# Merging each attention group with the image while the next groups run, in a four-layer image kernel on one core

## The chip, the cores and the metric

The kernel runs on one core of a Trainium2 chip. The metric is device microseconds of one execution; the kernel before takes 5507.82 us, the median of 3 runs (5503.45 to 5507.88).

## What is computed

The input x has 2 images of 128 channels, 128 rows (h) and 128 columns (w), in float32. Four layers follow each other, each on the group-normalised output of the one before, and each added to it (pre-activation residual):

```python
x = x + axial_attention(_gn(x))      # layer 0: along h, for every column w
x = x + four_line_scans(_gn(x))      # layer 1: down, up, right, left
x = x + deformable_conv(_gn(x))      # layer 2
x = x + hadamard_conv(_gn(x))        # layer 3
```

The change is in layer 0 and at the start of layer 1. Layer 0, for each of the 256 columns (image n, column w) and each of 8 groups of 16 channels:

```python
qkv = _bn(einsum('bgch,gdc->bgdh', xg, wg))             # q, k: 8 channels, v: 16
stacked = _bn(concat([qk, qr, kr]))                     # logits: q*k, q*embedding, k*embedding
sim = softmax(stacked.sum(over the three terms))
sv  = einsum('bgij,bgcj->bgci', sim, v)                 # "sums"
sve = einsum('bgij,cij->bgci', sim, v_emb)              # "embedded"
so  = _bn(concat([sv, sve]))                            # statistics per channel, over all columns and rows
out = so.reshape(N, W, 128, 2, H).sum(axis=3)           # sv and sve of a channel added
```

`_bn` of the output takes its mean and variance per channel over both images. A channel belongs to one group, so a group's output scales are known as soon as that group is done for both images. Layer 1 then takes the group norm of x + out (statistics over the whole image, 4 channels together) and runs four scans of 128 lines: each line is the line of the input plus the relu of a 9-tap convolution of the line before.

## The kernel before

The program is written for a tile framework. Where an engine is wrapped in `InOrder` (the helper of line 81, to which most instructions are put down in the profile), its instructions run in the order of the Python code; elsewhere the framework's scheduler picks the order. Matrix multiplies run on PE, vector work on DVE, activations on ACT, elementwise work also on POOL; DMAs are issued by SP in its own program order, a few by ACT.

**Preparing (`layer0_prepare`, line 92).** After the statistics, the last part (from line 493) loops over 32 blocks of four rows. Each step t makes q and k by position for the moments of the logits (`positions`, `against_embeddings`), and from t = 4 to t = 32 it also issues `project`: one matmul `ps_q` of 128x512, and two ACT activations of it into `sa` and `sb`; there are 64 projections, two to three a step, `ps_q` has two PSUM buffers. Every 4 projections `sb` goes to DRAM (`qb`, 1 MB), every 8 `sa` goes to DRAM (`qa`, 2 MB). The scales of the logits (`alphas`) come after the last step.

**Attention (`layer0_attention`, line 612).** A unit is 32 columns of one image and one group; there are 64 units (2 images, 8 groups, 4 blocks of 32 columns), with the image as the outermost loop. A unit is done in four pairs of 8 columns. The loop over m (line 865) runs 256 pairs and 15 more turns that drain the pipeline; turn m issues, in this order: logits of pair m (PE `lg`, then DVE `e<-lg,r`), the first half of the turning of pair m-2 (PE `te`, DVE `et<-te`), the maxima of pair m (DVE `mx`), the division of pair m-1 (DVE reciprocal of `total`, POOL `e<-e,total`), values of pair m-3 (PE `po`, ACT `svt<-po`), terms of the next unit (PE `gen`, ACT and DVE `r<-gen`), the embedded sums of pair m-7 (PE `po`, ACT `ste<-po`), the second half of the turning, the copy by position (POOL `et<-et`), and the 8 exponentials of pair m (ACT `e<-e,mx`). DVE's `bn_stats` of `svt` and `ste` follow, four for each unit. At the end of a turn come SP's transfers: at m % 4 == 3 the loads of `zz` (16 DMAs of 16 KB, two buffers) and `vt` for the unit after the next, and the stores of `svt` and `ste` (4 DMAs each) of finished units; at m % 4 == 0 the loads of `qk` (4 DMAs).

**Merging (`Merge`, line 929).** `Merge.begin` is called when the last logits are issued; `Merge.run` (line 1007) follows when attention has ended: `scales` makes the two factors and the shift per channel, then 8 blocks of 32 columns are read back from DRAM, scaled (ACT `u`), added (DVE `te`), added to the image in SBUF (`res`, half on DVE, half on POOL) and measured by `bn_stats` (DVE).

**First scan (`layer1`, line 1101).** `res` is stored to DRAM (`x1_d`, 34 DMAs), copied there once more by blocks of columns (`x1c_d`, 64-byte pieces, needed by the fourth scan alone), the group norm's scales are made, and scan d = 0 runs from row 0 to row 127, with rows normalised by ACT four rows ahead.

Of the kernel before, what the change touches and what calls it, by code (L numbers as in the profile page):

```python
# [16 lines left out]
N = 2  # L17
# [74 lines left out]
def layer0_prepare(env, x, prm, mem, alphas):  # L92
# [10 lines left out]
    with ExitStack() as ctx:  # L103
# [389 lines left out]
        with ExitStack() as part:  # L493
# [35 lines left out]
            def against_embeddings(t, zs):  # L529
# [20 lines left out]
                nc.gpsimd.tensor_tensor(acc, acc, prod, ALU.add)  # L550
# [26 lines left out]
            wait = 4  # L577
            zs_last = None
            for t in range(NT + 1):
                zs = positions(t) if t < NT else None  # L580
                if t >= wait:
                    share = -(-len(todo) // (NT + 1 - t))
                    for n, wc, b in todo[:share]:
# [5 lines left out]
                        if b % 4 == 3:  # L589
                            nc.sync.dma_start(  # L590
                                out=mem["qb"][:, n, wc, b // 4 * 2 : b // 4 * 2 + 2], in_=sb
                            )
                        if b == NB - 1:
                            nc.sync.dma_start(out=mem["qa"][:, n, wc], in_=sa)
# [17 lines left out]
def layer0_attention(env, prm, mem, alphas, mv, then):  # L612
# [20 lines left out]
    with ExitStack() as ctx:  # L633
# [7 lines left out]
        pp = ctx.enter_context(tc.tile_pool(name="at_ps", bufs=1, space=PSUM))  # L641

        st_v, st_e = (
            cp.tile([P, NG, N * NC, 2, 6], F32, name=f"st_so{k}", tag=f"st_so{k}")
# [3 lines left out]
        nc.scalar.dma_start(out=ve, in_=prm["vemb"])  # L648
# [3 lines left out]
        for j in range(2):  # L652
            nc.gpsimd.memset(zz[j].rearrange("p t i b w -> p (t i b w)"), 0.0)
        qk = zp.tile([P, 2, HW, S], F32, name="qk", tag="qk")
        po = pp.tile([P, 256], F32, name="po", tag="po")
        nc.vector.memset(po, 0.0)
        po_v = po.rearrange("p (q i) -> p q i", q=2)
        po_e = po.rearrange("p (i w) -> p i w", w=WC)

        qb = mem["qb"].rearrange("(t g c) n e s i b w -> g n e (s i) c t (b w)", t=2, g=NG)  # L660
        qa = mem["qa"].rearrange(
            "(t g c) n e (q r x) h -> t g c n e r q (x h)", t=2, g=NG, r=2, x=RT
        )
        sv = mem["sv"].rearrange("(g c) n e (q x) h -> g x c n e q h", g=NG, x=RT)
        sve = mem["sve"].rearrange("(g c) n e (s i) w -> g s c n e (i w)", g=NG, s=4)

        units = [(n, g, wc) for n in range(N) for g in range(NG) for wc in range(NC)]
# [4 lines left out]
        def load(at):  # L672
# [4 lines left out]
            for i in range(16):  # L677
                sync.dma_start(
# [8 lines left out]
        def load_qk(u):  # L687
            for t in range(2):
                for r in range(2):
# [3 lines left out]
                        in_=qa[t, u.g, :, u.n, u.wc, r],  # L693
                    )

        def terms_pe(u, t, k):
# [15 lines left out]
        def terms_copy(u, t, k, ps, s):  # L712

            part = slice(0, 1) if s == 0 else slice(1, 4)
# [4 lines left out]
            if s == 0:  # L719
                dve.tensor_scalar(to, here, scale, None, ALU.mult)  # L720
            else:
                act.activation(to, here, AF.Copy, scale=scale)
# [29 lines left out]
        def add_term(u, p, lg):  # L752
            e = ep.tile([P, 2 * RT, S], F32, name="e", tag="e", bufs=4)
# [48 lines left out]
        def values(u, p, et):  # L802
# [10 lines left out]
            if p == 0:  # L813
                u.sv = sp.tile([P, 2 * RT, S], F32, name="svt", tag="svt")
            act.copy(u.sv[:, 2 * p : 2 * p + 2, :], po_v)
# [19 lines left out]
        def store_sv(u):  # L835
            for x in range(4):
                sync.dma_start(out=sv[u.g, x, :, u.n, u.wc], in_=u.sv[32 * x : 32 * x + 16])

        def store_sve(u):
            for s in range(4):  # L840
                sync.dma_start(
                    out=sve[u.g, s, :, u.n, u.wc],
# [3 lines left out]
        def stats(u, st, t, half):  # L846
            dve.bn_stats(
                st[:, u.g, u.n * NC + u.wc, half, :],
                t.rearrange("p a b -> p (a b)")[:, 512 * half : 512 * half + 512],
# [7 lines left out]
        for at in range(2):  # L857
            us[at] = load(at)
            load_qk(us[at])
        for t in range(2):  # L860
            for k in range(2):
                ps = terms_pe(us[0], t, k)
                for s in (0, 1):
                    terms_copy(us[0], t, k, ps, s)
        for m in range(pairs + 15):
            here = m < pairs
            if m == pairs:
                early.close()
                then()
# [18 lines left out]
            if nxt and here:  # L888
                ps = terms_pe(nxt, p // 2, p % 2)
                for s in (1, 0):  # L890
                    terms_copy(nxt, p // 2, p % 2, ps, s)
# [1299 lines left out]
```

## Time and profile before

| | |
|---|---|
| median of 3 runs | 5507.82 us |
| profiled execution, its own time | 5498.68 us |
| its span | 5496.8 us |
| busy over the span | PE 94%, DVE 67%, ACT 49%, POOL 28% |
| first `gen` matmul, first `lg` matmul of attention | 399.8 us, 420.8 us |
| last `mx` of attention | 1892.3 us |
| last statistics of attention done | 1919.8 us |
| first matmul of the first scan | 2060.0 us |
| last matmuls of the four scans | about 3690 us |

A profile is one execution. A row of a timeline gives the start, the duration, the engine, the output and inputs, and in brackets how long the engine had been idle and who released it. A row of a stretch gives, for each engine, busy time and the number of instructions, then the share of full clock that PE was granted, the mean busy share of the 16 DMA engines and the rate. Busy times of pipelined instructions overlap a little, so the distance between starts is often shorter than the duration.

### The profile page before, as it was taken

Reading aid. Unit: us, or ns where it says so; the run is one execution under the profiler, and the core shown is the slowest. Engines: PE = TensorE matmul, PEld = TensorE weight load, DVE = VectorE, ACT = ScalarE, POOL = GpSimd, SP = SyncE. Lnnn points to the kernel's source line nnn. Section 1 sums busy time; section 2 is a strip of 40 time slices with the busy share of each in tenths; the row PEclk is TensorE's granted clock in tenths of the full one; section 3 lists DMA queues with packets and bytes.
Section 4 is the critical chain, followed back from the end, with each engine's and each line's share of the span. In section 5 each row is a group of like instructions: output and inputs, shape, how many; then the busy total and the mean of one; then the engine's idle time right before and its main releaser. Section 6 shows DMA issues by size and latency. Waiting matters only on the chain. (4 is left out here: it accounts for less than half of the span.)

```text
span 5496.8 us, 172767 instructions
## 1 busy us (share of the span) xinstructions
PE 5176.2 (94%) x72443; PEld 4608.0 (84%) x72443; DVE 3663.1 (67%) x7010; ACT 2672.4 (49%) x8182; POOL 1565.9 (28%) x1235
## 2 busy tenths in 40 slices
PE   7889999999999809999999999999899999999999
PEld 6757888888888709999999999984799999999877
DVE  3637888888888775555555556653566666666788
ACT  3558998888888745552223320013233333333332
POOL 3215666666666641000000003330000000000476
PEclk8999999999999859999999999999999999999999
DMA  4352333333333399900000001004667666666111
GB/s 162 136 234 52 61 61 61 61 61 61 61 61 61 96 366 167 93 1 1 1 1 1 1 1 47 32 34 122 110 88 88 88 88 87 88 88 88 41 55 55
DMA packets 673354, 421.04 MB, mean 77 GB/s; under 512 B 325696, under 2 KB 630720, under 8 KB 660672
## 3 DMA queue, kind: packets, MB, share of 16 engines
q1 hardware_dynamic: 667406, 400.69, 38.8%
q8 instruction: 580, 9.50, 0.7%
q10 hardware_dynamic: 5170, 9.23, 0.5%
q14 instruction: 198, 1.62, 0.1%
HBM read 269.09 MB, written 157.45 MB: 78 GB/s over the span
## 5 line engine op out<-in xcount | busy, mean ns | idle before, releaser
L81 PE MATMUL pl<-ln,wl 128*128 128x128 f32 (+1 forms) x10160 | 1240.7, 276 | 9.4 <-DVE ln L81 7.9
L81 PEld LDWEIGHTS pl<-ln,wl 128*128 128x128 f32 x10160 | 1175.7, 190 | 22.3 <-issue 6.6
L81 ACT ACTIVATE e<-e,mx 128x128 f32<-128x128 f32 x2048 | 793.4, 395 | 0.8 <-DVE mx L81 0.8
L81 ACT COPY sm<-ps_s 128x432 f32<-128x432 f32 (+1 forms) x768 | 318.2, 487 | 833.3 <-PE ps_s L81 808.9
L81 ACT COPY res<-ln 128x64 f32<-128x64 f32 (+1 forms) x1016 | 283.9, 304 | 701.5 <-DVE ln L81 701.5
L81 POOL TENSOR_TENSOR e<-e,total 128x1024 f32<-128x1024 f32 x256 | 485.6, 1897 | 486.3 <-DVE total L81 481.4
L81 DVE COPY s<-ps_w 100x1152 f32<-100x1152 f32 x256 | 346.3, 1353 | 333.4 <-PE ps_w L81 326.6
L81 POOL TENSOR_TENSOR res<-ln,x1t 128x128 f32<-128x128 f32 x256 | 148.9, 582 | 1428.7 <-DVE ln L81 1428.7
L81 PE MATMUL ps_s<-s,xw 100*128 100x144 f32 x4096 | 546.5, 287 | 6.6 <-DMA xw<-px_d 6.6
L81 PE MATMUL po<-sm,wdef 128*128 128x256 f32 x2304 | 539.2, 379 | 0.0
L81 PE MATMUL pl<-ln,ws 128*128 128x128 f32 x4064 | 536.8, 273 | 0.0
L81 POOL COPY et<-et 128x1024 f32<-128x1024 f32 x256 | 517.2, 2020 | 34.9 <-DVE et L81 26.1
L81 PEld LDWEIGHTS ps_s<-s,xw 100*128 100x128 f32 x4096 | 518.5, 191 | 7.1 <-DMA xw<-px_d 7.0
L81 DVE TENSOR_TENSOR v<-pl,c 128x128 f32<-128x128 f32 x508 | 148.0, 291 | 540.5 <-PE pl L81 537.3
L81 PEld LDWEIGHTS pl<-ln,ws 128*128 128x128 f32 x4064 | 494.5, 190 | 0.0
L81 ACT ACTIVATE r<-gen,alphas 128x1536 f32<-128x1536 f32 x256 | 394.9, 1542 | 172.3 <-PE gen L81 144.2
L81 PEld LDWEIGHTS po<-sm,wdef 128*128 128x128 f32 x2304 | 419.8, 190 | 47.6
L81 POOL MEMSET col<- 128x10 f32 (+1 forms) x72 | 5.9, 122 | 1460.6 <-DVE res L81 1453.0
L81 ACT ACTIVATION_READ_ACCUMULATOR e<-e,mx 128x1 f32 x2048 | 396.8, 194 | 0.0
L81 DVE SCALAR_TENSOR_TENSOR ln<-v,res 128x128 f32<-128x128 f32 x1016 | 346.4, 341 | 48.5 <-POOL res L81 0.9
L81 PE MATMUL te<-cst_main,e 128*128 128x128 f32 x2048 | 338.6, 288 | 24.0 <-POOL e L81 16.7
L81 PE MATMUL gen<-zz,toep 32*128 32x128 f32 x8192 | 334.1, 288 | 23.2 <-DMA zz<-qb_d 15.2
(247 smaller groups left out, 9118.8 us busy)
## 6 DMA issues: line engine op xcount, KB each, us to landing
xw<-px_d SPq DMA_DIRECT2D x1275, 80.0 KB
xa<-in_x SPq DMA_DIRECT2D x16, 1024.0 KB
v_d<-vs SPq DMA_DIRECT2D x16, 1024.0 KB
qb_d<-sb SPq DMA_DIRECT2D x16, 1024.0 KB
qa_d<-sa SPq DMA_DIRECT2D x8, 2048.0 KB
zz<-qb_d SPq DMA_DIRECT2D x1024, 16.0 KB
vt<-v_d SPq DMA_DIRECT2D x64, 256.0 KB
qk<-qa_d SPq DMA_DIRECT2D x256, 64.0 KB
```

Of the source, the lines that this page charges most:

```text
L81: return lambda *a, **k: self.tc.keep_in_program_order(issue(*a, **k))
```

## The change

In attention the group becomes the outermost loop (`units`), so that a group is complete for both images after 32 pairs. A new method `Merge.slot(m, ...)` is called at the end of every turn m. For group g it issues, from turn 32g + 43 on, the scales of that group in five steps (two small DVE operations; a matmul into 4 columns of `po`; four DVE operations; a square root on ACT; five DVE operations), and then, for 7 of the 8 groups, eight chunks (image, 32 columns) at a distance of three turns: loads of `te`, `tv` and of the image chunk `t` into SBUF, one ACT activation of 128x512, three POOL operations of 128x512, one DVE `bn_stats`, and the store of the merged chunk to `x1_d`. The last group is merged after attention in `Merge.finish`. `Merge.norm` makes the group norm's scales from the statistics by group. `res` isn't filled any more by merging: `layer1` loads it row block by row block from `x1_d`.

The DRAM tensors change their layout: `qa`, `qb` and `x1_d` have image and block before the channel; `sv` has pieces of 16 floats where it had 128, so that the channels of a group and eighths of the rows make 128 partitions; `te`, `tv` are read as 2 KB per partition, the image chunk in pieces of 32 floats. The projections are done in turns 4 to 27, three in a turn. The first unit's loads of `zz` are shared by the queues of SP and ACT, and its four `gen` results have two PSUM buffers and are copied whole, two by ACT, two by DVE. `e` has three buffers instead of four. In the first scan's first 48 lines the two operations that add the image row are issued per image.

```diff
-                nc.gpsimd.tensor_tensor(acc, acc, prod, ALU.add)
+                pool.tensor_tensor(acc, acc, prod, ALU.add)
...
-            wait = 4
+            wait, last = 4, NT - 4
+            pool = InOrder(tc, nc.gpsimd)
             zs_last = None
             for t in range(NT + 1):
                 zs = positions(t) if t < NT else None
-                if t >= wait:
-                    share = -(-len(todo) // (NT + 1 - t))
+                if wait <= t < last:
+                    share = -(-len(todo) // (last - t))
...
-                                out=mem["qb"][:, n, wc, b // 4 * 2 : b // 4 * 2 + 2], in_=sb
+                                out=mem["qb"][n, wc, :, b // 4 * 2 : b // 4 * 2 + 2], in_=sb
...
-                            nc.sync.dma_start(out=mem["qa"][:, n, wc], in_=sa)
+                            nc.sync.dma_start(out=mem["qa"][n, wc], in_=sa)
...
+        sv = mem["sv"].rearrange("g n e c r q x h -> g n e x c (r q) h")
+        sve = mem["sve"].rearrange("g n e c (s i) w -> g n e s c (i w)", s=4)
...
+        units = [(n, g, wc) for g in range(NG) for n in range(N) for wc in range(NC)]
...
+        def load(at, queues=(sync,)):
...
+                queues[-1 if i % 3 == 2 else 0].dma_start(
...
-            e = ep.tile([P, 2 * RT, S], F32, name="e", tag="e", bufs=4)
+            e = ep.tile([P, 2 * RT, S], F32, name="e", tag="e")
...
-            act.copy(u.sv[:, 2 * p : 2 * p + 2, :], po_v)
+                u.sv = sp.tile([P, 8, 2 * RT, 16], F32, name="svt", tag="svt")
+            act.copy(
+                u.sv[:, :, 2 * p : 2 * p + 2, :].rearrange("p r q h -> p q r h"),
+                po_v.rearrange("p q (r h) -> p q r h", r=8),
+            )
 
...
-            us[at] = load(at)
+            us[at] = load(at, (sync, act) if at == 0 else (sync,))
             load_qk(us[at])
-        for t in range(2):
+        nc.scalar.dma_start(out=ve, in_=prm["vemb"])
+        merge.begin(prm)
+        with tc.tile_pool(name="at_p0", bufs=2, space=PSUM) as first:
             for k in range(2):
-                ps = terms_pe(us[0], t, k)
-                for s in (0, 1):
-                    terms_copy(us[0], t, k, ps, s)
+                for t, engine in ((0, act), (1, dve)):
+                    ps = terms_pe(us[0], t, k, first)
+                    terms_copy(us[0], t, k, ps, slice(0, 4), engine)
...
+            if m == 4 * len(units) + 7:
+                merge.load_last(1, False)
+            merge.slot(m, po[:, 256:260])
...
+        merge.slot(pairs + 15, po[:, 256:260])
+        merge.finish()
...
+    def scales(self, g, step, ps):
+        dve, mv, vec = self.dve, self.mv[:, g], self.vec[:, g]
+        if step == 1:
+            sq = self.tile([P, 2], "sq_out")
+            dve.tensor_tensor(sq, mv[:, :, 0], mv[:, :, 0], ALU.mult)
+            dve.tensor_tensor(mv[:, :, 1], mv[:, :, 1], sq, ALU.add)
+        elif step == 2:
+            self.pe.matmul(
+                ps, lhsT=self.gather, rhs=mv.rearrange("p k m -> p (k m)"), start=True, stop=True
+            )
+        elif step == 3:
+            self.a = self.tile([P, 2], "a_out", 2)
+            self.b = self.tile([P, 2], "b_out", 2)
+            self.m = self.tile([P, 2, 2], "m_out", 2)
+            self.shift = self.tile([P, 1], "shift", 2)
+            m = self.m
+            dve.tensor_copy(m.rearrange("p k m -> p (k m)"), ps)
+            dve.tensor_tensor(self.b, m[:, :, 0], m[:, :, 0], ALU.mult)
+            dve.tensor_tensor(self.a, m[:, :, 1], self.b, ALU.subtract)
+            dve.tensor_scalar(self.a, self.a, float(EPS_BN), None, ALU.add)
+        elif step == 4:
+            self.act.activation(self.a, self.a, AF.Sqrt)
+        elif step == 5:
+            a, b = self.a, self.b
+            dve.reciprocal(a, a)
+            dve.tensor_tensor(a, a, vec[:, 0:2], ALU.mult)
+            dve.tensor_tensor(b, a, self.m[:, :, 0], ALU.mult)
+            dve.tensor_tensor(b, vec[:, 2:4], b, ALU.subtract)
+            dve.tensor_tensor(self.shift, b[:, 0:1], b[:, 1:2], ALU.add)
...
+    def slot(self, m, ps):
+        cols = lambda wc: slice(wc * WC, (wc + 1) * WC)
+        for g in range(NG):
+            at = m - 32 * g - 42
+            if 1 <= at <= 5:
+                self.scales(g, at, ps)
+            if g == NG - 1:
+                continue
+            for k in range(N * NC):
+                n, wc = k // NC, k % NC
+                step = at - 6 - 3 * k
+                if step == -3:
+                    te = self.sp.tile([P, 16, WC], F32, name="te_x", tag="te_x")
+                    self.sync.dma_start(out=te, in_=self.embedded(g, n, wc))
+                    tv = self.sp.tile([P, WC, 16], F32, name="tv_x", tag="tv_x")
+                    self.sync.dma_start(out=tv, in_=self.sums(g, n, wc))
+                    self.chunks[g, k] = [te, tv]
+                elif step == -2:
+                    t = self.sp.tile([P, 16, WC], F32, name="t_x", tag="t_x")
+                    self.sync.dma_start(out=t, in_=self.x[g, n, :, :, cols(wc)])
+                    self.chunks[g, k].append(t)
+                elif step == 0:
+                    te, tv, t = self.chunks[g, k]
+                    self.act.activation(
+                        te, te, AF.Identity, bias=self.shift, scale=self.a[:, 1:2]
+                    )
+                    self.pool.tensor_tensor(
+                        tv, tv, self.a[:, 0:1].unsqueeze(2).to_broadcast([P, WC, 16]), ALU.mult
+                    )
+                elif step == 1:
+                    te, tv, t = self.chunks[g, k]
+                    self.pool.tensor_tensor(t, t, te, ALU.add)
+                elif step == 2:
+                    te, tv, t = self.chunks[g, k]
+                    self.pool.tensor_tensor(t, t, tv.rearrange("p w h -> p h w"), ALU.add)
+                elif step == 3:
+                    t = self.chunks.pop((g, k))[2]
+                    self.dve.bn_stats(self.st[:, g, n, wc, :], t.rearrange("p h w -> p (h w)"))
+                    self.aggregate(g, n, wc)
+                    self.sync.dma_start(
+                        out=self.x1[g, n, :, :, cols(wc)],
+                        in_=t,
+                    )
+    def aggregate(self, g, n, wc):
+        if wc == NC - 1:
+            self.dve.bn_aggr(self.mx[:, g, n, :], self.st[:, g, n].rearrange("p t k -> p (t k)"))
+    def load_last(self, n, first):
+        g = NG - 1
+        if first:
+            tc = self.env.tc
+            self.lp = self.ctx.enter_context(tc.tile_pool(name="mg_l", bufs=2, side="right"))
+            self.last = {}
+            for k in range(N):
+                t = self.lp.tile([P, 16, S], F32, name="xl", tag="xl")
+                self.sync.dma_start(out=t, in_=self.x[g, k])
+                self.last[k] = [t]
+        te = self.lp.tile([P, NC, 16, WC], F32, name="tel", tag="tel")
+        tv = self.lp.tile([P, NC, WC, 16], F32, name="tvl", tag="tvl")
+        for wc in range(NC):
+            self.sync.dma_start(out=tv[:, wc], in_=self.sums(g, n, wc))
+            self.sync.dma_start(out=te[:, wc], in_=self.embedded(g, n, wc))
+        self.last[n] += [te, tv]
+    def finish(self):
+        g = NG - 1
+        def stats(n, wc):
+            t = self.last[n][0]
+            self.dve.bn_stats(self.st[:, g, n, wc, :], t[:, :, wc * WC : (wc + 1) * WC])
+            self.aggregate(g, n, wc)
+        before = None
+        for n in range(N):
+            t, te, tv = self.last[n]
+            for wc in range(NC):
+                here = t[:, :, wc * WC : (wc + 1) * WC]
+                self.act.activation(
+                    te[:, wc], te[:, wc], AF.Identity, bias=self.shift, scale=self.a[:, 1:2]
+                )
+                self.dve.scalar_tensor_tensor(
+                    here,
+                    tv[:, wc].rearrange("p w h -> p h w"),
+                    self.a[:, 0:1],
+                    here,
+                    ALU.mult,
+                    ALU.add,
+                )
+                self.pool.tensor_tensor(here, here, te[:, wc], ALU.add)
+                if before is not None:
+                    stats(*before)
+                before = n, wc
+            self.sync.dma_start(out=self.x1[g, n], in_=t)
+        stats(*before)
...
+    def norm(self, to):
...
-                nc.sync.dma_start(out=x1_d[:, n, lo:hi, :], in_=res[n][:, lo:hi, :])
+                nc.sync.dma_start(out=res[n][:, lo:hi, :], in_=x1_d[n, :, lo:hi, :])
...
-                        dve.tensor_copy(new[k], here[k])
+                        for n in range(N):
+                            row = res[n][:, line, k::2] if d == 0 else here[k][:, n]
+                            dve.tensor_copy(new[k][:, n], row)
...
+                def rectified(k, v):
+                    if d == 0 and at < 48:
+                        for n in range(N):
+                            row = res[n][:, line, k::2]
+                            dve.scalar_tensor_tensor(
+                                new[k][:, n], v[:, n], 0.0, row, ALU.max, ALU.add
+                            )
+                    else:
+                        dve.scalar_tensor_tensor(new[k], v, 0.0, here[k], ALU.max, ALU.add)
...
-        "qa": dram.tile([P, N, NC, WC, S], F32, name="qa_d", tag="qa_d"),
-        "qb": dram.tile([P, N, NC, 4, 4, 8, WC], F32, name="qb_d", tag="qb_d"),
+        "qa": dram.tile([N, NC, P, WC, S], F32, name="qa_d", tag="qa_d"),
+        "qb": dram.tile([N, NC, P, 4, 4, 8, WC], F32, name="qb_d", tag="qb_d"),
...
-        "sv": dram.tile([P, N, NC, WC, S], F32, name="sv_d", tag="sv_d"),
-        "sve": dram.tile([P, N, NC, S, WC], F32, name="sve_d", tag="sve_d"),
+        "sv": dram.tile([NG, N, NC, 16, 8, 8, RT, 16], F32, name="sv_d", tag="sv_d"),
+        "sve": dram.tile([NG, N, NC, 16, S, WC], F32, name="sve_d", tag="sve_d"),
...
```

## Prediction

> **What bounds the kernel now.** I read the page's slices first, then busy time by stage, the waits inside attention, and the timelines of the two seams, where attention starts and where the first scan starts. The slices:
>
> ```profile
> PE   7889999999999809999999999999899999999999
> ...
> DMA  4352333333333399900000001004667666666111
> ```
>
> A slice is 137.4 us. PE is at work nearly everywhere; the one empty slice, where the DMA is full, is merging. The stages:
>
> ```profile
> 421.00:1893.00 1472.00, 1429.43 (x36208) 1203.12 (x36209) 1261.57 (x1786) 1312.70 (x4835) 988.95 (x507) 1.00 0.32 59
> 1893.00:1919.00 26.00, 16.15 (x548) 11.13 (x537) 10.75 (x19) 7.74 (x28) 10.83 (x6) 0.55 0.79 292
> 1919.00:2060.00 141.00, 1.16 (x4) 1.00 (x4) 105.80 (x144) 68.67 (x39) 54.63 (x18) 0.50 0.90 356
> ```
>
> Columns after the length: PE, PEld, DVE, ACT, POOL. From 1919 to 2060 us PE works 1.2 us: merging is bare, nothing lies beside it. In attention (1472 us, 256 pairs, 5.75 us each) ACT is busy 89%, DVE 86%, POOL 67%, the DMAs 32%; no engine is full. Waits in 1000 to 1400 us (70 pairs), each with total, count and longest:
>
> ```profile
> POOL e L81 <- DVE total L81: 120.0, 69, 2.4
> DVE r L81 <- ACT r L81: 47.8, 68, 1.3
> ACT r L81 <- PE gen L81: 39.7, 70, 1.7
> ```
>
> So a pair is a ring through four in-order engines, in which ACT waits 0.57 us, DVE 0.70 us and POOL 1.74 us. The seams:
>
> ```profile
> 399.81 0.76 PE L81 MATMUL gen<-zz,toep 32*128 32x128 f32 x2 [12.03 <-DMA zz<-qb_d]
> ...
> 420.81 1.97 PE L81 MATMUL lg<-cst_main,r 128*128 128x128 f32 x8
> ...
> 1919.82 0.17 DVE L977 TENSOR_TENSOR sq_out<-mv_out 128x16 f32<-128x16 f32 x1
> ...
> 1944.61 1.23 DVE L81 TENSOR_TENSOR res<-te,res 128x1024 f32<-128x1024 f32 x1 [11.84 <-DMA res<-in_x]
> ...
> 2060.03 3.83 PE L81 MATMUL pl<-ln,wl 128*128 128x128 f32 x20 [3.70 <-DVE ln L81]
> ```
>
> **What the skill says.** SBUF — State Buffer, "Who interferes with whom": a DVE operation with both inputs in SBUF and a GpSimd operation that reads SBUF exclude each other; a reduction doesn't contend. The trace agrees: in the first scan DVE's `ln<-ln,ln` (both inputs in SBUF) takes 0.29 us alone and 0.70 beside POOL's weight sums from 2096 us on. In attention every DVE addition has one input in PSUM, and DVE's `mx` keeps 1.21 us beside POOL. DMA: Bandwidth & Descriptors, "Specifications", puts line rate at 512 B and more; here 64-byte copies (`x1c_d`) keep the queue full at 91 GB/s from 2060 us on. ScalarE: Activation LUTs, "What ACT_TABLE_LOAD costs", gives about 2.66 us for a switch of sets, drain included; the trace shows 1.28 us (`ACT_TABLE_LOAD`, 428.13 to the first exponential at 429.43), and I use that.
>
> **Start of attention: -11 us.** Projections are spread over 24 turns instead of 29, by the share's formula 16 turns with three and 8 with two, where there were 6 and 23. The spacing of POOL's `acc` shows 6.11 us for a turn with three (PE waits 0.59 us for ACT to free a `ps_q` buffer), 4.40 with two and about 2.7 with none. Before: 6 x 6.11 + 23 x 4.40 = 138; after: 16 x 6.11 + 8 x 4.40 + 5 x 2.7 = 146.5. So `alphas`, at 389.5 us, come at 398. In return the 3 MB of stores that keep `zz` waiting until 399.8 are out before. `zz` still needs its buffer, zeroed by POOL (1.80 us) when the image is read for the last time, at about 391 after the change; 16 loads over two queues land near 400. Then ACT and DVE each copy two results of 2048 columns (ACT about 2.05, from 1.54 for 1536; DVE about 2.6, from 0.75 for 512) against four rounds of 0.75 + 1.54 one after the other: `lg` near 410 instead of 420.8. Bounds: -4 (DMA late) to -18.
>
> **Merging leaves the bare stretch: -111 us.** Of 1919.8 to 2060.0 there remain: scales, 3.4 us as before (1919.82 to 1923.2); eight chunks of the last group, in which DVE's 512 columns (0.68, half of the 1.28 of `te<-te,a_out,u`) and POOL's 512 columns (1.26, as `ws<-wl`) have both inputs in SBUF and so go in turn, 8 x 1.95 = 15.6, plus 1.5 to fill; statistics and group norm 4.5 (3.7 from 2055.0 to 2058.7, plus own and reduce); beside that, the 1 MB store of the chunk and the load of the first rows, about 8 us after the last addition; 1.3 for normalising. That is 3.4 + 17.1 + 8 + 1.3, about 30, with `pl` near 1949. The other loads of `res` (16 MB at the 356 GB/s of merging: 47 us) run ahead of a scan that takes 3.13 us a row. Bounds: -95 to -120.
>
> **Seven groups merge inside attention: +56 us.** A group adds to ACT: 8 activations of 128x512 (0.7, as `sb<-ps_q`) = 5.6, a square root 0.2, two table loads 2.6, together 8.4. To DVE: 8 `bn_stats` at a spacing of 0.60, 2 small aggregates of 0.3, 11 tiny operations of 0.2, together 7.6. PE gets one tiny matmul. If nothing hides, 7 x 16.0 = 112. If all goes into the waits above (ACT 144.2 us on `gen`, DVE 173.2 on `r` over the stage), 0. The kernel before shows what a `bn_stats` costs in the ring: the distances of DVE's `e` are 6.13 us in a turn with two, 5.23 and 5.72 with one, 5.46 with none, so four cost 22.5 - 21.8 = 0.7, or 0.17 of 0.60 each. But ACT's activation falls into the same turn as DVE's statistics, and a table load before the exponentials meets no wait. I take half, 56.
>
> **POOL: +5.** A chunk adds one operation a turn: 1.1 (broadcast factor, from 1.90 for 1024), 1.26 and 1.26. POOL waits 1.74 us a pair for `total`; in the shortest turns (5.2) that leaves nothing over, so 168 operations cost 0.03 each on average. If they took the 3.45 us per 1024 of merging they would exceed the wait by 0.5 each, 84 us; but there DVE's operations had two SBUF inputs. Behind POOL's extra operation waits the next division, and PE's turning waits for that.
>
> **SP's queue: +17.** This is the step that I can bound least. Before, SP issues `zz` as soon as the last `gen` has read the buffer:
>
> ```profile
> 971.96 7.22 SPq L81 DMA_DIRECT2D zz<-qb_d  x16
> 986.65 0.34 SPq L81 DMA_DIRECT2D vt<-v_d  x1
> ```
>
> and it is needed at about 999, four turns later. Now a chunk's store precedes it in the queue, and the store waits until POOL has done the addition of the turn before, 1.6 us into the turn. With the store in the turn just before (2 of 6 units in a group's window, by the order of SP's instructions), the store and two loads (1.0), 16 `zz` (7.2, as above) and landing (about 2.5), `zz` lands about 12.4 us after that turn's start, where `gen` comes 11.2 us after it: 14 waits of 1.2 us. The pieces of 64 bytes (4096 a unit) and 128 bytes (4096 a chunk) fill the DMAs further; at the rate of the 64-byte copies (262144 in about 218 us) they are 3.4 us each, beside the 32% of 23 us that are used. Bounds: 0, and 5 us in each of the 42 units, 210.
>
> **First scan: +3.** PE is the bound (14 matmuls, 3.13 us a line; DVE waits 1.14 us for `pl`). The split operation adds about 0.1 us twice a line in 47 lines, which that wait hides; where POOL's weight sums slow DVE (about five lines of 3.58), some of it shows. Without cover 47 x 0.2 = 9. Three `e` buffers cost nothing: `e` of m-3 is read for the last time before `lg` of m on PE, and `e` waits for `lg`. The layouts of `qa`, `qb`, `x1_d` change the addresses alone; the fourth scan's `x1c_d` has 1200 us.
>
> **Sum.** -11 - 111 + 56 + 5 + 17 + 3 = -41: the span goes from 5496.8 to 5456, the profiled execution from 5498.7 to 5458. The median of the runs lies 9.1 us above that execution, so 5507.8 becomes 5467.
>
> **Rivals.** (1) *The work hides entirely.* For it: every engine has waits, and `bn_stats` costs little. Against it: seven times two table loads. With 15 us paid in attention: -11 - 111 + 15 + 3 = -104, near 5404 to 5440. (2) *SP becomes the bound in the merged groups, and `zz` takes the place of merging.* Place: `gen` at the first pair of a unit, waiting for `zz`, with ACT `r` behind it. For it: SP issues 28 transfers in a turn with `zz`, 10 us and more, and a wait at a chunk's store holds all of them. Price: 3 us in 42 units is 126 in place of 17, so +68: 5576. It decides from 1.4 us a unit on (58 us). Against it: the slack of the other four units in six. (3) *Half of the seam's gain stays away*: rows wait for the stores, POOL and DVE exclude each other longer, attention pays nearly everything: 5485 to 5500.
>
> **How the numbers follow.** Forecast 0.45, hidden 0.25, SP 0.17, half 0.13. Less than 0.2%, 11 us, can't be told from no change. Faster: forecast, hidden and most of the half, 0.78; same 0.05; slower 0.17. The likeliest case alone reaches from 5440 to 5490. The range of 8 in 10 takes in most of the hidden case and the milder SP case: 5415 to 5535.
>
> **What would show it.** First `lg` near 410; turns in the merged groups 5.9 to 6.1 us instead of 5.75; POOL near 80% there; `gen<-zz` waiting for DMA about 17 us in all, not over 60; 30 us with PE idle between the last statistics of attention and `pl`; lines of the first scan still 3.13. The prediction is wrong if merged turns exceed 6.3 us, or if the first scan waits for rows.

## The result, and the profile after

The changed kernel takes 5550.96 us (median of 4 runs, 5545.29 to 5557.18) against 5505.64 us for the kernel before (4 runs, 5499.97 to 5507.88): 1.0082 times the time before, 95% interval 1.0070 to 1.0094. It is slower by 45 us, where 41 us less were forecast. The profiled executions have spans of 5496.8 and 5555.4 us; they lie 58.6 us apart, 13 us more than the medians, so a difference between stages of two executions is sure to some 10 us at best. By stage:

| stage | before | after | difference | forecast |
|---|---|---|---|---|
| start to the first `lg` | 420.8 | 419.1 | -1.7 | -11 |
| attention: first `lg` to the last `mx` | 1471.5 | 1608.8 | +137.3 | +78 |
| last `mx` to the last statistics of attention | 26.9 | 50.1 | +23.2 | not priced |
| from there to the first matmul of the first scan | 140.8 | 32.8 | -108.0 | -111 |
| the four scans | 1628.9 | 1634.6 | +5.7 | +3 |
| the rest | 1807.9 | 1810.0 | +2.1 | 0 |

The forecast of attention is the sum of the steps "seven groups", "POOL" and "SP's queue". The slices of the page after, where the empty one is gone and the DMAs are busier in attention:

```profile
PE   7889999999899967999999999999899999999999
...
DMA  4353355555555569900000000104676666677211
```

The stages, with the columns as before (length; PE, PEld, DVE, ACT, POOL; granted clock; DMA share; GB/s):

```profile
421.00:2028.00 1607.00, 1491.64 (x36162) 1247.60 (x36162) 1328.21 (x1927) 1369.40 (x4908) 1182.86 (x665) 0.96 0.53 89
2028.00:2078.00 50.00, 14.58 (x580) 10.44 (x580) 14.20 (x25) 10.47 (x32) 23.90 (x17) 0.59 0.79 190
2078.00:2111.00 33.00, 1.14 (x5) 1.21 (x6) 23.12 (x50) 8.72 (x17) 12.15 (x10) 0.50 0.59 200
```

Merging's bare stretch did shrink to 33 us, but attention is 137 us longer, although ACT (busy 85%) and DVE (83%) are less full than before and only POOL is fuller (74%, where it was 67%). And PE's granted clock, 1.00 before, is 0.96. The waits in 1000 to 1400 us, in which now 63 pairs fit instead of 70:

```profile
POOL e L81 <- DVE total L81: 59.4, 41, 3.8
DVE r L81 <- ACT r L81: 57.9, 52, 5.2
ACT r L81 <- PE gen L81: 49.2, 52, 5.5
...
PE gen L81 <- DMA zz<-qb_d: 9.0, 11, 1.3
```

The longest waits of ACT and DVE have grown from 1.7 and 1.3 us to more than 5: the ring of engines stops now and then. The two seams, the start of attention and the start of the first scan:

```profile
409.40 3.43 PE L81 MATMUL gen<-zz,toep 32*128 32x128 f32 x58 [6.05 <-DMA zz<-qb_d]
...
419.09 1.23 PE L81 MATMUL lg<-cst_main,r 128*128 128x128 f32 x5 [2.64 <-DVE r L81]
...
2078.59 0.16 DVE L81 TENSOR_TENSOR sq_out<-mv_out 128x2 f32<-128x2 f32 x1
...
2110.85 2.48 PE L81 MATMUL pl<-ln,wl 128*128 128x128 f32 x10 [9.22 <-DVE ln L81]
```

**Where in attention.** The distance from one of DVE's `mx` to the next gives the length of a turn; a group has 32 turns, counted from 0. The first group, in which nothing is merged, takes 185.4 us (183.4 before). The other seven hold nearly all of the loss, and it sits in few turns:

| seven groups | before | after | difference |
|---|---|---|---|
| turns 3 to 5 | 120.7 | 156.3 | +35.6 |
| turns 11 to 15 (the scales) | 204.6 | 234.9 | +30.3 |
| turns 27 to 29 | 116.7 | 152.8 | +36.1 |
| the other 21 | 840.7 | 874.2 | +33.5 |

Turn 4 takes 9.2 to 13.5 us in six of the seven groups, turn 28 9.9 to 11.5 us in six of the seven, where 5 to 7 are usual. Here is SP's queue ahead of such a turn 4 (start, duration of the issue with its waits, and the transfer):

```profile
1024.10 2.01 SPq L81 DMA_DIRECT2D x_d<-t_x  x1
1026.20 2.81 SPq L81 DMA_DIRECT2D te_x<-sve_d  x1
1029.06 0.43 SPq L81 DMA_DIRECT2D tv_x<-sv_d  x1
1029.59 5.54 SPq L81 DMA_DIRECT2D zz<-qb_d  x16
```

A chunk's store and loads stand before `zz` and take 5.4 us; SP is done with `zz` at 1035.1, while `gen` begins to read it at 1033.9 and then waits twice. What PE then does, in a turn 28:

```profile
1185.85 0.46 PE L81 MATMUL gen<-zz,toep 32*128 32x128 f32 x2 [0.50 <-DMA zz<-qb_d]
1187.40 2.04 PE L81 MATMUL gen<-zz,toep 32*128 32x128 f32 x26 [1.09 <-DMA zz<-qb_d]
```

```profile
1188.00:1200.00 12.00, 12.00 (x230) 10.08 (x226) 5.86 (x9) 6.65 (x21) 6.22 (x4) 0.50 0.63 84
1204.00:1210.00 6.00, 6.00 (x167) 5.00 (x160) 5.28 (x9) 5.16 (x20) 5.05 (x4) 1.00 0.35 74
```

PE waits 1.6 us, and then its clock is granted at 0.50 for 13.7 us, from 1187.2 us on (the record of the clock goes in steps of 3.4 us): 26 matmuls of `gen` take 2.04 us there, 32 of them 1.17 us later. Between 480 and 1890 us the record has 113 us at 0.50; before the change it has none there. In attention the waits for `zz` are these (total, count, longest):

```profile
PE gen L81 <- DMA zz<-qb_d: 30.0, 40, 1.6
PEld gen L81 <- DMA zz<-qb_d: 14.8, 20, 1.4
```

In turns 3 to 5 and 27 to 29 PE's own waits for `zz` add to 27.0 us, and the stretches at half clock that begin there to 92 us. As an estimate, half clock loses half of its length, 46 us; together that is 73 us, and these turns are 71.7 us longer. So most of the price of a late `zz` was paid after the wait.

SP itself: from 1000 to 1400 us the rows of its timeline, with the waits inside a row, add to 245 us before and 357 us after; the issues alone to 179 and 331 us. Part of that is new transfers (51 us), but a store of `sv` rose from 0.54 to 1.12 us, of `sve` from 0.51 to 0.83, a load of `qk` from 0.34 to 0.80 (means over the rows).

### The profile page after: what moved, and what is told of

It reads as the page before. It is cut to its first block, busy times and chain, and to the rows that moved or that the text cites. A ratio compares the mean times of both kernels' runs of the same rounds, so it can differ in the third digit from the quotient of the medians.

```text
span 5555.4 us, 173579 instructions
## 1 busy us (share of the span) xinstructions
PE 5243.4 (94%) x72457; PEld 4656.5 (84%) x72457; DVE 3663.0 (66%) x7161; ACT 2671.2 (48%) x8233; POOL 1729.5 (31%) x1395
## 5 line engine op out<-in xcount | busy, mean ns | idle before, releaser
L81 ACT ACTIVATE e<-e,mx 128x128 f32<-128x128 f32 x2048 | 793.5, 395 | 14.1 <-DVE mx L81 13.7
L81 ACT ACTIVATE r<-gen,alphas 128x1536 f32<-128x1536 f32 (+1 forms) x254 | 392.5, 1545 | 203.9 <-PE gen L81 203.8
L81 PE MATMUL gen<-zz,toep 32*128 32x128 f32 x8192 | 361.2, 297 | 38.2 <-DMA zz<-qb_d 36.6
L81 DVE SCALAR_TENSOR_TENSOR ln<-v,res 128x128 f32<-128x128 f32 (+1 forms) x1110 | 357.1, 329 | 48.9 <-POOL res L81 0.9
```

The costliest lines, as they stand in the source:

```text
L81: return lambda *a, **k: self.tc.keep_in_program_order(issue(*a, **k))
```

## Experiments

Ratios are to the kernel before, with 95% intervals; the changed kernel has 1.0082. "Waits for `zz`" are those of `gen` on PE and on its weight loads together, from the first `lg` to the last `mx`: 2.1 us before the change, 44.8 us after it. "At half clock" counts 480 to 1890 us. Stages and turns come from one execution of each run.

### zz three turns earlier

Theory S: SP issues `zz` too late, and the stop costs more than itself. Theory E: the added work on the engines lengthens the turns.

```diff
-            if m % 4 == 3 and m // 4 + 2 < len(units):
-                us[m // 4 + 2] = load(m // 4 + 2)
+            if m % 4 == 0 and m // 4 + 2 < len(units):
+                us[m // 4 + 2] = load_zz(m // 4 + 2)
+            if m % 4 == 3 and m // 4 + 2 < len(units):
+                load_v(us[m // 4 + 2])
```

> The loads of zz for the unit after next are put in SP's queue three turns earlier (turn 4u instead of 4u+3); nothing else moves. Theory S (SP issues zz too late, the generated terms wait, and TensorE's granted clock then halves for some 7 to 14 us): turns 4 and 28 of a merged group fall from 10 to 13 us to about 6, the waits of the generated terms for zz go from about 45 us to under 5, the stretches at half clock in the attention from about 116 us to under 40, and the time to about 5490 us (60 less). Theory E (the added work on POOL, DVE and ACT is what lengthens the turns): 5545 to 5551 us, the long turns stay long.

5514.8 us, 1.0016 (1.0009 to 1.0024): 36 us of the 45 are back, where theory S expected 60. Turns 27 to 29 sum to 122.4 us, no `gen` waits for `zz` any more, 48 us are at half clock. Turns 3 to 5 remain at 146.9, and now `lg` waits:

```profile
PE lg L81 <- DMA qk<-qa_d: 20.5, 16, 5.1
```

`qk` stands behind `zz` in SP's queue. The engines' work and the DMAs' share (0.54, changed kernel 0.53) are as they were, so the order of SP's queue is shown as a cause; but in part the lateness has moved and not gone.

### The chunks' transfers on ACT's queue

```diff
-                    self.sync.dma_start(out=te, in_=self.embedded(g, n, wc))
+                    self.act.dma_start(out=te, in_=self.embedded(g, n, wc))
...                 # tv, t and the store likewise
```

> The four transfers of each chunk (te_x, tv_x, t_x, x_d) are issued by ACT instead of SP: the same traffic, and 56 x 4 issues less on SP. Theory S, with SP's order as the cause: the waits for zz mostly go and turns 4 and 28 shorten, 5500 to 5520 us, since ACT pays about 2.5 us a chunk for the issues. If it is the traffic and not SP's order that makes zz late: the waits for zz stay at 30 to 45 us, and with ACT's issues the time rises to 5560 to 5620 us. Theory E: slower, 5570 us or more, as ACT is a busy engine.

5682.3 us, 1.0324 (1.0305 to 1.0343), and the waits for `zz` rise to 160 us. The time lies above what theory S expected in either form, and in the range of theory E alone; but the waits of SP's own queue (640 to 1890 us) show a cause that none of them had:

```profile
SPq L81 <- DMA x_d<-t_x: 232.3, 37, 10.8
SPq L81 <- DMA t_x<-in_x: 130.7, 42, 6.9
SPq L81 <- DMA te_x<-sve_d: 93.0, 31, 12.3
```

SP's issues waited 456 us until transfers issued by ACT had landed; in the changed kernel such a wait for `x_d` is 17.3 us. The trace's record of the issues shows how. The program's transfers signal eight semaphores in rotation, an issue waits until the last transfer on its semaphore has landed, and here SP and ACT share the eight: a `zz` at 1303.64 us waits on the semaphore that `te_x`, issued by ACT at 1298.68, has to signal. So the two queues are coupled by the program's semaphores, and the run tells neither traffic from order nor theory E from theory S. A transfer given to another queue did not leave SP's.

### Chunks without arithmetic, chunks without loads

In the first run the activation and POOL's three operations are left out; in the second the three loads are, and the arithmetic works on a constant matrix. Groups 0 to 6 of the merged image then do not hold the layer's output.

> The chunks' arithmetic inside the attention is left out (the activation on te_x and POOL's three operations); its loads, its stores, its statistics and the scales stay, so that groups 0 to 6 of the merged image are the bare image. Theory E (the engines' added work): merged turns fall to about 5.8 us except for the scales' turns, 5551 falls by 60 to 90 us to about 5475 us. Theory S: the late loads of zz stay, with turns 4 and 28 at 9 us or more, and the time falls by 10 to 35 us only.

5512.6 us, 1.0011 (1.0002 to 1.0020), 38 us less than the changed kernel: just above what theory S expected, far from theory E's 60 to 90. But S missed too, for it expected turn 28 to stay long: turns 27 to 29 fall to 122.4 us, while turns 3 to 5 fall only to 144.4 and turns 11 to 15 stay at 236.0.

> The chunks' three loads (te_x, tv_x, t_x) are left out; their arithmetic, on a constant, their stores, statistics and scales stay (groups 0 to 6 of the merged image are then not the image). Theory S in either form: turns 4 and 28 fall to about 6 us, the waits for zz nearly go, the time falls by 45 to 65 us to about 5495 us. Theory E (engines): 5540 us or more, and turns 4 and 28 stay at 10 us.

5461.3 us, 0.9930 (0.9913 to 0.9947). That is 90 us less than the changed kernel, more than the 45 to 65 that theory S expected. With all arithmetic in place turns 3 to 5 and 27 to 29 are back at 120.1 and 123.8 us, and the waits for `zz` at 0.8. Theory E falls for these turns. That turns 27 to 29 came back without the arithmetic too is open to this reading, which no run isolates: in the changed kernel SP's queue waits 67.7 us for POOL's operations on `t_x` (640 to 1890 us), up to 14.7 us at once, with everything behind it. Such waits alone do not make `zz` late: without the loads they are 131.8 us, and SP has the time for them.

### Stores of 512 bytes, and both remedies

```diff
-        sv = mem["sv"].rearrange("g n e c r q x h -> g n e x c (r q) h")
+        sv = mem["sv"].rearrange("g n e c r x q h -> g n e x c r (q h)")
```

POOL's addition of `tv` reads the tile in that order; in `finish` DVE's step becomes four of 128x128.

> The sums over values are stored in pieces of 512 bytes instead of 64 (the memory's order is c, r, x, q, h instead of c, r, q, x, h; POOL's addition and the last group's step read the tile in that order). SP's four stores of sv took 4.4 to 5 us a unit in the changed kernel, 1.7 to 2.3 in the one before. Theory S1 (SP is late because the new layouts make its issues long): the four stores take about 2 us again, SP gains 2.5 us a unit, the waits for zz fall to under 20 us, the time to 5505 to 5525 us. Theory S2 (SP is late because it waits in order behind the chunks' stores and loads): stores shorten, but turns 4 and 28 stay long, 5540 to 5551 us.

5507.0 us, 1.0004 (0.9997 to 1.0011): a store of `sv` takes 0.72 us on SP instead of 1.12, of `sve` 0.61 instead of 0.83; waits for `zz` 15.9 us; turns 3 to 5 129.4, turns 27 to 29 131.9 us. That is as S1 expected, and 44 us of the loss hang on the one layout. Two things stay open. The DMAs are relieved as well (their share from 1000 to 1400 us falls from 0.57 to 0.53), so that the time on SP and the traffic go together here. And the pieces of `sve` are what they were, so an issue's length did not depend on its own pieces alone.

> Stores of 512 bytes as in the run sv512, and zz of the unit after next issued at turn 4u+1 (behind the loads of qk, two turns earlier than in the changed kernel). Theory S: no wait for zz or qk above 5 us in all, turns 4 and 28 at about 6 us, half-clock stretches in the attention under 20 us; 5475 to 5495 us, under the kernel before. If the waits that stay in the run with early zz come from something other than SP's order: 5505 to 5515 us, as there.

5478.1 us, 0.9957 (0.9941 to 0.9972): faster than the kernel before. SP's queue, at about the same turns:

```profile
1039.36 2.91 SPq L81 DMA_DIRECT2D qk<-qa_d  x4
1042.83 0.60 SPq L81 DMA_DIRECT2D x_d<-t_x  x1
1043.53 7.08 SPq L81 DMA_DIRECT2D zz<-qb_d  x16
1053.21 0.34 SPq L81 DMA_DIRECT2D vt<-v_d  x1
```

SP is no longer behind: it stands 2.6 us between `zz` and `vt`, until the buffer of `vt` is free. Attention, with practically the same instructions on every engine as in the changed kernel:

```profile
421.00:1950.00 1529.00, 1439.57 (x36162) 1207.32 (x36162) 1325.85 (x1926) 1368.88 (x4907) 1182.42 (x665) 0.99 0.49 94
```

The waits for `zz` are 0.2 us, 10 us are at half clock, turns 3 to 5 and 27 to 29 are at 119.9 and 122.1 us. Attention takes 1531.2 us, 59.7 more than before the change: so, by these two executions, the merging itself costs 59.7 us, and SP's lateness, with all that follows from it, 77.6 us. The run without the chunks' loads, where SP is in time for another reason, has 1528.0 us in attention and agrees.

### What a stop of the ring costs

To separate the stop from its aftermath, the kernel *before* gets four more maxima on DVE ahead of the first copy of turned blocks, in each of 8 turns:

```diff
                 te = turn(e, 0)
+                if m % 32 == 20:
+                    for _ in range(4):
+                        maxima(es[m])
                 turned(et, 0, te)
```

> The kernel before, with four more maxima on DVE ahead of the first copy of turned blocks in every 32nd turn (8 turns in all; nothing else changes). They take 4 x 1.13 = 4.5 us, of which DVE's own wait in a turn can hide up to 1.3. If a stall costs only itself, these turns are 3.2 to 4.5 us longer and the time rises by 26 to 36 us. If TensorE's granted clock halves after the stall, as the changed kernel's trace suggests, each is followed by a stretch of 3.4 to 7 us at half clock, the turn and the next are 6 to 8 us longer together, and the time rises by 48 to 64 us.

5559.9 us, 1.0095 (1.0078 to 1.0112). The insertion, and the stretches around it (columns as before):

```profile
541.79 4.60 DVE L81 TENSOR_REDUCE mx<-e 128x8 f32<-128x1024 f32 x4
```

```profile
530.00:541.00 11.00, 10.58 (x277) 8.79 (x271) 9.19 (x15) 9.87 (x37) 7.35 (x5) 1.00 0.55 103
541.00:547.00 6.00, 1.86 (x96) 1.62 (x91) 5.97 (x7) 2.46 (x6) 0.51 (x1) 0.83 0.20 42
547.00:557.00 10.00, 9.96 (x151) 8.41 (x152) 6.09 (x9) 4.87 (x18) 5.64 (x3) 0.59 0.01 2
557.00:567.00 10.00, 10.00 (x282) 8.37 (x281) 8.69 (x12) 9.29 (x39) 5.97 (x4) 1.00 0.39 81
```

Attention takes 1529.6 us in this execution, 58.1 more, 7.3 us for each insertion; by the medians the kernel is 54 us slower, 6.8 us for each. PE itself stands for 3.1 to 4.2 us each time. In the ten microseconds after it PE does 151 matmuls instead of 282, at a granted clock of 0.59. All eight stops are followed by 6.8 to 10.2 us at half clock (78.5 us in all, none at these places without the insertion). So an insertion of 4.6 us is paid about one and a half times, as the expectation with the halved clock had it.

### The scales' small operations on POOL

```diff
-            dve.tensor_tensor(self.b, m[:, :, 0], m[:, :, 0], ALU.mult)
+            pool.tensor_tensor(self.b, m[:, :, 0], m[:, :, 0], ALU.mult)
```

and eight more of the kind. In the changed kernel DVE's operation on 2 columns ends when POOL's does:

```profile
1096.27 1.98 DVE L81 TENSOR_TENSOR b_out<-m_out 128x2 f32<-128x2 f32 x1
```

```profile
1096.23 1.99 POOL L81 COPY et<-et 128x1024 f32<-128x1024 f32 x1 [0.32 <-DVE m_out L81]
```

It takes 1.98 us where its neighbours take 0.16. The first product of the scales takes 1.47 us and one more 0.80, and they too end when POOL's running copy does.

> The scales' small operations that read two operands from SBUF are on POOL instead of DVE; the order stays. Theory P (on DVE they wait, 0.8 to 2 us each, until POOL's running operation ends, and the turns behind them are long by 4.7 us a group): turns 11 to 15 of a merged group sum to about 30 us instead of 33.5, and the time falls by 15 to 30 us to about 5528 us. If the long durations on DVE only fill time in which DVE would wait anyway: 5551 us, within 5 us.

5541.7 us, 1.0063 (1.0046 to 1.0080). Turns 11 to 15 sum to 217.1 us, 17.8 less, so theory P holds for them; of that 9 us reach the total, less than the 15 to 30 expected.

### The end of attention

In the drain of the changed kernel the last statistics of `ste` wait in DVE's order behind the chunks' `st_x`:

```profile
2063.62 0.69 DVE L81 BATCH_NORM_STATS2 st_x<-t_x 128x6 f32<-128x512 f32 x1 [13.48 <-POOL t_x L81]
...
2076.38 0.69 DVE L81 BATCH_NORM_STATS2 st_x<-t_x 128x6 f32<-128x512 f32 x1 [10.89 <-POOL t_x L81]
...
2077.96 0.59 DVE L81 BATCH_NORM_AGGREGATE mv_out<-st_so 128x2 f32<-128x96 f32 x1
```

The next run brings group 6's chunks closer together, with SP as it is; the second does so with the two remedies above, the third with the small operations on POOL as well.

```diff
-                step = at - 6 - 3 * k
-                if step == -3:
+                apart = 2 if g == NG - 2 else 3
+                step = at - 6 - apart * k
+                if step == -apart:
...
-                elif step == -2:
+                elif step == 1 - apart:
```

> Group 6's chunks start two turns apart instead of three, so that its last chunk ends before the attention's last turn and not among the short turns behind it. Theory T (behind the last turn the chunks' transfers take 9 to 13 us each, and the last group's statistics wait in DVE's order behind the chunks' statistics): last turn to the first scan matmul 60 us or less instead of 83, time about 5528 us. Rival: the same work then lengthens group 6's turns as much, and the time stays within 6 us of 5551.

5557.8 us, 1.0100 (1.0078 to 1.0123). The stretch from the last `mx` to the last statistics is 27.3 us, as before the change, which shows that the chunks among the short turns lengthened it. But attention grows by 21.5 us, one turn takes 20.2, and nothing is won, about as the rival said. In front of that turn SP stands at the load of the last group's image:

```profile
2026.32 0.58 SPq L81 DMA_DIRECT2D x_d<-t_x  x1
2038.05 0.35 SPq L81 DMA_DIRECT2D xl<-in_x  x1
2038.51 0.61 SPq L81 DMA_DIRECT2D t_x<-in_x  x1
```

> The run sv512_zz with group 6's chunks two turns apart. Theory T once more, now with SP relieved: in the run tail2 the last turns of the attention waited for late loads (20.2 us in one turn); with SP in time they should not, so that the last turn to the first scan matmul falls from 76 to about 55 us and the time from 5478 to about 5458 us. Rival: the closer chunks lengthen the last turns by as much as the tail gains: 5473 to 5483 us.

5481.0 us, 0.9959 (0.9947 to 0.9972), no gain over 5478.1: the stretch falls from 39.4 to 29.8 us, attention rises by 7.1, and in this execution the first `lg` came 4 us later. The rival was right.

> As the run zz_sv_tail, and the scales' small operations with two SBUF operands on POOL, as in the run tiny_pool. There turns 11 to 15 took 217 us in seven groups instead of 235. Theory P: 10 to 18 us less than zz_sv_tail, 5440 to 5450 us. Rival: POOL, now with 3.9 us more a chunk in a ring without stalls, passes its delay on to the turned blocks: no gain over zz_sv_tail.

5471.3 us, 0.9939 (0.9922 to 0.9956): turns 11 to 15 sum to 219.2 instead of 235.1 us. The gain over the run before, 10 us, is just what theory P expected at least, though the two intervals overlap; the time is 21 us above the one it named. It is 34.6 us faster than the kernel before and 80 us faster than the changed one.

The last two runs move the last group's loads (`load_last`) nine and three turns later.

```diff
             if m == pairs:
                 early.close()
+            if m == pairs + 9:
                 merge.load_last(0, True)
```

> In the changed kernel the last group's loads (xl, tvl, tel) stand nine turns later in SP's order, behind group 6's last chunk. Theory L (the load of xl waits in SP's queue for attention's buffers, 10 us with SP idle, and group 6's last chunks and the stores of sv and sve wait behind it): from the last maxima to the attention's last statistics about 30 to 38 us instead of 50.1, 5535 to 5543 us. Rival (the chunks' own transfers are slow among the short turns, whatever stands in front of them): 47 to 51 us there, and the late loads of xl then add up to 10 us before the first scan: 5551 to 5561 us.

5546.4 us, 1.0074 (1.0057 to 1.0091), and 44.5 us instead of 50.1. The edit did less than meant: `tvl` and `tel` moved, but the scheduler left the first load of `xl` ahead of the chunk, at 2016.1 us. So theory L is neither shown nor refuted.

> The run zz_sv_tail_tiny with the last group's first loads three turns later in SP's order, behind the close chunks of group 6. Theory L: the last turns of the attention (6.9 to 8.2 us in that run) fall back to 5.5 to 6.2, 6 to 10 us in all, and the time goes from 5471 to about 5463 us. Rival: these turns are long by the doubled arithmetic of the chunks; 5468 to 5474 us.

5469.3 us, 0.9943 (0.9922 to 0.9965): the last turns are still at 6.9, 7.7 and 7.6 us; no difference to 5471.3.

### The start

```diff
-            wait, last = 4, NT - 4
+            wait, last = 4, NT + 1
```

> In the changed kernel the projections are spread over turns 4 to 32 again, as before the change; all else stays. If the earlier end of the projections is worth what the prediction gave it (the 3 MB of stores out of the way of zz), the first logits come 8 to 11 us later than 419.1 and the time rises to about 5560 us. If the start is bound by something that both have (the zeroing after the last read of the image, then 16 loads of zz that land one behind the other), the first logits come within 3 us of 419 and the time stays at 5551 us, within 5 us.

5545.5 us, 1.0072 (1.0054 to 1.0089); the first `lg` comes at 420.5 us, so undoing the spread loses nothing that can be seen. In the thirteen executions with the new start the first `lg` comes between 414.6 and 425.6 us, in the two with the old one at 420.8 and 422.1. So the -1.7 us of the table can't be told from nothing, and the start is bound by something that both have.

## Why the prediction was wrong, step by step

**SP's queue (+17)** is the step that failed. Its place was right, and so was its mechanism (a chunk's store ahead of `zz`), but it was sized at 17 us and measured 77.6. Three things were not in the sum. First, the durations of SP's issues were taken from the kernel before: "the store and two loads (1.0)" took 5.4 us ahead of the turn 4 shown above. Of `qa` and `qb` the prediction said that the layouts "change the addresses alone", but a load of `qk` took 0.74 to 0.80 us in six runs with the new layout, 0.34 before; of `sv` it counted the 64-byte pieces as traffic, not as time on SP. (Its rate for such pieces was near: the 64-byte copies of the kernel before run from 2094 us on, not from 2060, at 87 to 89 GB/s for the most part instead of 91, and take 208 us instead of 218.) Second, it counted 14 waits of 1.2 us; there are twelve long turns, and PE's own waits for `zz` are 1.1 to 2.6 us in each, 23 us in all. Third, and largest in time, a wait was priced at its own length, while the stretches at half clock behind the waits add about 46 us by the estimate above. Rival 2 had named this place, with a deciding point of 58 us; SP's share passed it. Its 126 us were too much.

**Seven groups (+56) and POOL (+5)**: 59.7 us in the run without lateness against 61. The sum is right, its terms less so, and that they cancel is luck. Half of what was measured, 30 us, lies in the scales' five turns. There "11 tiny operations of 0.2" took 5.5 us a group instead of 2.2, 23 us more in seven groups: three of them wait for POOL. The Trainium skill (SBUF — State Buffer, "Who interferes with whom") says that a DVE instruction with two SBUF inputs contends with a GpSimd instruction that reads SBUF, and the trace agrees (1.98, 1.47 and 0.80 us instead of 0.16); the prediction applied that to merging and to the scan, and overlooked it here. POOL's operations measured 1.04, 1.28 and 1.54 us (forecast 1.1, 1.26, 1.26), ACT's 0.81 (0.7). Outside these five turns some 29 us remain of the 79 that the chunks' activations and statistics add to ACT and DVE, so more than half is hidden, which makes up for the scales.

**Merging leaves the bare stretch (-111)**: 32.8 us remain where 30 were forecast, -108.0. What failed is that this was taken for the whole seam: the drain in front of it was assumed unchanged, and takes 23.2 us more, since three chunks of group 6 fall among turns of 2 to 4 us, and there the statistics of one follow those of the one before after 13 to 17 us.

**Start (-11)**: -1.7. `alphas` come at 402.4 us (398 forecast), `zz` is zeroed at 396.2 (forecast about 393), and its 16 loads have landed at 409.4, 13 us later; "land near 400" is the term that was off. From there to `lg` it took the 10 us of the forecast.

**First scan (+3)**: +5.7 over the four scans; PE's weight loads wait 9.3 us for POOL's weight sums (`ws`), one candidate for the difference. No run tests it.

The sum of the measured terms is -1.7 + 137.3 + 23.2 - 108.0 + 5.7 + 2.1 = 58.6, the difference of the spans. Of what the prediction named as signs, the turns (6.15 to 6.51 us by group, where over 6.3 was to count against it) and the start spoke against it; POOL at 74% and the 33 us did not.

## What to carry to other kernels

Treat a queue that issues in order as an engine: sum its load with the durations that the *new* transfers have and with the waits of each store for its producer, and put loads with a deadline in front of stores without one. Piece size can count twice, on the DMAs and on the issuing queue: 512 bytes instead of 64 gave 44 us here, and the run does not split the two. Before a transfer is given to another queue, look at what the issues wait for. Work moved under a pipeline also has to be priced where the pipeline drains, 23 us here; ending it earlier only moved that cost. And a stop in a ring that keeps PE full should be priced with the clock that follows it.

## What the runs showed of the hardware

- After stops of PE of 3.1 to 4.2 us the granted clock was 0.50 for 6.8 to 10.2 us (all eight inserted stops); once, after waits of 0.5 and 1.1 us, for 13.7 us.
- Four stores of 1024 pieces of 64 bytes kept SP 1.12 us each, of 128 pieces of 512 bytes 0.72 us each, with the same bytes. The stores of `sve` behind them, whose pieces were the same in both runs, took 0.83 and 0.61 us.
- A DVE operation on two columns, both inputs in SBUF, was held until POOL's running operation ended, 1.98 us instead of 0.16.
